# Self-attention of a decoder layer: first loads in halves, SyncE in source order, keys and values of cross-attention from step 2 to 58

## The chip, the cores and the metric

The kernel runs on one core of a Trainium2 chip. Its metric is the device time of one execution in microseconds (us). Each core has TensorE (PE, matrix products), VectorE (DVE), ScalarE (ACT), GpSimd (POOL) and SyncE (SP), which here only issues DMA transfers. Each of these runs its instructions in one fixed order. Where an instruction waits, all that is behind it on that engine waits too, and this holds for the DMA issues of SyncE and GpSimd as well.

## The reference, cut to what matters

All is fp32, with 8 batch rows of 256 tokens and 1024 features.

```python
def reference(x, ctx, pos, mask, ...):
    x = layernorm(x + self_attention(x))            # 32 heads of 32, 8 key/value heads, rope, causal
    x = layernorm(x + cross_attention(x, ctx, pos, mask))   # 32 heads of 128, 8 key/value heads, rope by pos
    x = layernorm(x + ffn(x))                       # a router with 256 slots, top 8
    return x

def self_attention(h):
    q, k, v = h @ wq.T, h @ wk.T, h @ wv.T
    q, k = q * cos + rotate_half(q) * sin, k * cos + rotate_half(k) * sin
    att = softmax(q @ k.T / sqrt(32) + causal)      # 4 query heads share a key head
    return (att @ v) @ wo.T

def cross_attention(h, ctx, pos, mask):
    q, k, v = h @ Wq, ctx @ Wk, ctx @ Wv
    q, k = rope(q, table[pos]), rope(k, table[pos])
    att = softmax(where(mask == 0, -1e9, q @ k.T / sqrt(128)))
    return (att @ v) @ Wo
```

## The kernel before

**Stages.** The kernel has three: self-attention with its layer norm, cross-attention with its own, and the feed-forward part. The change touches the first. In it, cross-attention's keys and values, which need only ctx, are also made, so that TensorE has work while softmaxes run.

**Steps.** Self-attention is a loop of 64 steps, s = 8b + c, for batch row b and group c of four query heads. A step issues, in the order of the source: the weighted sum of the group (`weighted`, L332, in odd steps, for the pair of steps s-1 and s together); the scores of the next step (`scores`, L266, with the softmax of L283 on DVE, L288 and L294 on ACT, and the transposes L299 and L303 on DVE); the query projection of step s + 2 (`project` L207 with `rope` L217 to L220); and one part of `others`: for c < 4 the output projection of the row before (`project_out`, L366), else keys and values of the next row (L207 and L236), and for c of 5 and 6 the turning of the finished row for the next stage (L390). For row 0, c < 4 makes the keys and values of row 1. Values go through DRAM to be laid out anew: `values` writes sa_v rows on ACT's queue, `load_values` (L311) reads them back on SyncE.

**Cross-attention's products in the loop.** From step `KV_BEGIN` to `KV_END` (L32), each step has four products out of 224, which are 4 quarters of 512 tokens by 4 pairs of key/value heads by 14. A pair's product is made by seven products instead of eight, in the order p1, p2, p6, p5, p3, p7, p4, once for keys (L744, and L738 for the turned form) and once for values. p6 and a later one use sums of weights. Those are made on GpSimd: `sums_of_inputs` loads two halves of weights into "ws" (L428, 2 buffers), `run` combines them (four L416) and stores two sums to DRAM (L439), from where SyncE loads them like any weight (L108). `steps` (L478 and L479) says in which step each of these events stands. An event e loads its own half and combines the half of event e-1. `load_all_positions` (L670 for the gathers of the rope tables, L688 to L696 for the positions, made on DVE) and `xa_context(0)` (L629 to L636: ctx and its sums) stand at step KV_BEGIN - 2. `xa_tables` (L704 to L713) turns the tables.

**Buffers.** Weights for all of this share a ring of 9 buffers of 512 KB, and `self.weights` (L108) issues the load on SyncE where the source takes a buffer. xT, the input of a row, has two buffers of 1 MB, sa_v 2, sa_wo (output weights, `load_out`, L357) 4.

**What sets the order.** A scheduler (Tile) places the instructions of an engine by its own costs, except on the engines that `manual_schedule` names: these keep the order of the source. Before, these are TensorE and GpSimd (L97), so SyncE's loads stand where the scheduler puts them. `load_x` (L161) needs a buffer that row b - 1 has been read from for the last time.

**The prologue.** Before the loop: the first keys' weights and xT of row 0 (L178 to L179), then keys, query, values and scores for the first steps (L492 to L504).

Of the kernel before, what the change touches and what calls it, by code (L numbers as in the profile page):

```python
# [8 lines left out]
F32 = mybir.dt.float32  # L9
# [6 lines left out]
DRAM = bass.MemoryType.DRAM  # L16
PE = mybir.EngineType.PE
POOL = mybir.EngineType.Pool

P = 128  # L20
B, S, E = 8, 256, 1024
NT = B * S // P
KC = E // P
# [5 lines left out]
SA_D, SA_KV = 32, 8  # L29
SA_SCALE = 1.0 / SA_D ** 0.5  # L30
SA_STEPS = B * KC
KV_BEGIN, KV_END = 4, 60  # L32

XA_H, XA_KV, XA_D = 32, 8, 128
XA_SCALE = 1.0 / XA_D ** 0.5
# [35 lines left out]
class Layer:  # L71
# [16 lines left out]
    def run(self):  # L88
        nc = self.nc
        self.ident = self.const.tile([P, P], F32, name="ident")  # L90
        make_identity(nc, self.ident)
        self.neghalf = self.const.tile([P, 1], F32, name="neghalf")
        nc.gpsimd.memset(self.neghalf, -0.5)
        self.cos = self.const.tile([P, TQ], F32, name="cos")
        self.sin = self.const.tile([P, TQ], F32, name="sin")
        self.wsums, self.kT_d, self.v_d, self.tables_d = {}, {}, {}, {}
        with self.tc.manual_schedule(engines={PE, POOL}):  # L97
            self.self_attention()
        with self.tc.manual_schedule(engines={PE}):
            self.cross_attention()  # L100
# [45 lines left out]
    def self_attention(self):  # L146
# [4 lines left out]
        nc, tc, a, uni, small = self.nc, self.tc, self.a, self.uni, self.small  # L151
        main, early, psum = ExitStack(), ExitStack(), ExitStack()
        sp = self.pool("sa", 1, main)
        ep = self.pool("sa_early", 1, early, side="right")
        p_sc = self.pool("sa_sc", 2, psum, space=PSUM)

        xTs = {}

        def load_x(b):
            xTs[b] = ep.tile([P, KC, S], F32, name="xT", bufs=2)  # L160
            nc.sync.dma_start(out=xTs[b], in_=a["xT"][b])  # L161

        def load_residual(b):
            for t in (2 * b, 2 * b + 1):
# [7 lines left out]
        def load_kv(b, name):  # L172

            for i in range(2):
                src = a[name][:, :, i * P : (i + 1) * P] if name == "sa_wk" else a[name][:, 4 * i : 4 * i + 4, :]
                wkvs[b, name, i] = self.weights([P, *src.shape[1:]], src)

        load_kv(0, "sa_wk")  # L178
        load_x(0)  # L179
        nc.scalar.dma_start(out=rot, in_=a["sa_rot"])  # L180
        nc.scalar.dma_start(out=sin, in_=a["sa_sin"])
        nc.scalar.dma_start(out=cos, in_=a["sa_cos"])
# [1 line left out]
        def signed():  # L184

            ones = sp.tile([P, 1], F32, name="sa_ones")
            nc.gpsimd.memset(ones, 1.0)
            ps = self.mm()
            nc.tensor.matmul(ps[:, 0:1], lhsT=rot, rhs=ones, start=True, stop=True)
            sign = sp.tile([P, 1], F32, name="sign")  # L190
            nc.vector.tensor_copy(sign, ps[:, 0:1])
            nc.vector.tensor_scalar(sin, sin, sign, None, ALU.mult)
# [31 lines left out]
        def keys(b, i):  # L224
            if i == 0:
                kTs[b] = sp.tile([P, 2, S], F32, name="sa_kT", bufs=2)
                if b:
                    load_kv(b, "sa_wk")
            rope(kTs[b][:, i, :], project(wkvs.pop((b, "sa_wk", i)), xTs[b]))

        def values(b, tt):
            if b and tt == 0:
                load_kv(b, "sa_wv")
            ps = self.mm()
            for k in range(KC):
                nc.tensor.matmul(  # L236
                    ps[:, :256], lhsT=xTs[b][:, k, tt * P : (tt + 1) * P],
                    rhs=wkvs[b, "sa_wv", k // 4][:, k % 4, :],
                    start=(k == 0), stop=(k == KC - 1),
                )  # L240
            rows = sp.tile([P, SA_KV * SA_D], F32, name="sa_vrow", bufs=2)
            nc.scalar.copy(rows, ps[:, :256])
            if tt == 0:
                v_d[b] = self.dram.tile([S, SA_KV * SA_D], F32, name=f"sa_v_{b}")
            nc.scalar.dma_start(out=v_d[b][tt * P : (tt + 1) * P, :], in_=rows)
# [3 lines left out]
        def load_query(s):  # L249
            wqs[s] = self.weights([P, KC, P], a["sa_wq"][s % KC])  # L250

        def query(s):
            ps = project(wqs.pop(s), xTs[s // KC])
            qTs[s] = sp.tile([P, S], F32, name="sa_qT", bufs=2)
            rope(qTs[s], ps)
# [49 lines left out]
        def load_values(b, half):  # L305


            v = vs[b, half] = sp.tile([P, BLOCKS, 4 * SA_D], F32, name="sa_v", bufs=2)
            rows = v_d[b].rearrange("(c i) d -> i c d", i=32)[:, :, half * P : (half + 1) * P]
            for i in range(4):  # L310
                nc.sync.dma_start(out=v[32 * i : 32 * i + 32], in_=rows)  # L311
# [87 lines left out]
        def others(s):  # L399


            b, c = divmod(s, KC)
            parts = []
            if b and c < 4:
                parts.append(lambda: project_out(b - 1, c))
            elif c < 4 or 1 < b + 1 < B:
                parts.append([
                    lambda: keys(b + 1, 0), lambda: keys(b + 1, 1),
                    lambda: values(b + 1, 0), lambda: values(b + 1, 1),
                ][c % 4])  # L410
            if b and c in (5, 6):
                parts.append(lambda: turn(b - 1, c - 5))
            return parts
# [61 lines left out]


        n = XA_KV * 2
        steps = [1 + e * 7 // 8 for e in range(n)]  # L478
        steps += [15 + e * (KV_END - 17) // (len(sums) - n) for e in range(len(sums) - n + 1)]  # L479
        made = []  # L480

        def sum_event():
# [6 lines left out]
        self.hp, self.raws = ep, 3  # L489
        products = [part for q in range(NQ) for m in range(XA_KV // 2) for part in self.xa_keys_values(q, m)]  # L490

        signed()  # L492
        keys(0, 0)
        load_query(0)
        load_kv(0, "sa_wv")
        keys(0, 1)
        load_query(1)
        load_x(1)
        load_query(2)
        query(0)  # L500
        values(0, 0)
        query(1)
        scores(0)
        values(0, 1)  # L504
        last = SA_STEPS
        for s in range(last):
            b, c = divmod(s, KC)
            if c == 4:
                load_residual(b)
            if s == KV_BEGIN - 2:  # L510
                self.load_all_positions()
                self.xa_context(0)
            events = [sum_event] * steps.count(s)
            n = NQ * XA_KV // 2 * 14 // (KV_END - KV_BEGIN)
            mine = []
            if KV_BEGIN <= s < KV_END:
                mine, products = products[:n], products[n:]
            elif s == last - 2:
                mine, self.queries = self.queries[:4], self.queries[4:]
            elif s == last - 1:  # L520
                mine = self.queries + more[:3]
                more = more[3:]
            quarter, first = divmod((s - KV_BEGIN) * n, XA_KV // 2 * 14)
            first = first == 0 and KV_BEGIN <= s < KV_END

            def one():
                if mine:
                    mine.pop(0)()

            def event():  # L530
                if events:
                    events.pop()()

            if s == last - 1:

                for _ in range(5):
                    one()
            if s % 2:
                weighted(s, False)
            elif not first and s < last - 2:  # L540
                one()
            if s % 2 == 0 and s + 1 < last:
                scores(s + 1)
            if s + 2 < last:
                query(s + 2)
            while norms:
                norms.pop(0)()
            for part in others(s):
                part()
            event()  # L550
            one()
            if s % 2:
                weighted(s, True)
                one()
                if s + 1 < last:
                    scores(s + 1)
            if c < 2:
                load_values(b, c)
            elif c == 6:
                load_out(b, 0)  # L560
            if b and c == 1:
                load_out(b - 1, 1)
            if b and c == 0 and b + 1 < B:
                load_x(b + 1)
            if s + 3 < last:
                load_query(s + 3)
            while mine:
                one()
            while events:
                event()  # L570
            if first:
                self.xa_tables(quarter)
            left = len(products)
            if KV_BEGIN <= s < KV_END and left and left % (XA_KV // 2 * 14) == 0:
                self.xa_context(NQ - left // (XA_KV // 2 * 14))
            if s == last - 3:
                early.close()
                self.xa_early()
                more = self.xa_query(1)
            if s == last - 1:  # L580
                psum.close()
                self.xa_psum()
# [1009 lines left out]
```

## Time and profile before

| | |
|---|---|
| median of three runs | 3483.88 us (3478.9 to 3484.5) |
| profiled execution, its own time | 3477.49 us |
| its span in the profile | 3475.7 us |
| mean granted TensorE clock | 0.986 |
| TensorE busy | 3373.5 us, 97% |
| DVE, ACT, POOL busy | 2114.2, 1202.3, 1047.0 us |
| bytes over the span | 626.36 MB, mean 180 GB/s |

The profiled execution is one execution, and its time stands 6.4 us below the median. The span is what the trace covers of it. Busy times are sums over instructions, and those of one engine don't overlap. In the views that follow, a timeline row is start, duration, engine, line, operation and, in brackets, the idle time just before with what ended it. A wait row is the waiting engine and line, what it waited for, and total, times and longest in us. PEclk is the clock granted to TensorE, in tenths of full speed in the page and as a fraction of 1 in the table by windows.

The stage of self-attention ends near 1215 us of the span. The first product of cross-attention stands at 100.61 us.

### The profile page before, as it was taken

What the parts mean: (1) busy time and instruction counts of PE and PEld (TensorE: products, weight loads), DVE (VectorE), ACT (ScalarE), POOL (GpSimd) and SP (SyncE); (2) the same over time, 40 slices, a digit from 0 to 9 for tenths busy, and PEclk for the clock granted to TensorE, in tenths of its full rate; (3) what the DMA queues carried; (4) which work ended last, traced back from release to release, by engine and by line L of the source; (5) the groups of instructions that cost most, each with busy time, mean ns of one, the idle gap of its engine ahead of it and who ended that gap; (6) DMA issues with size and microseconds to landing.
All of it is one profiled execution on the core that took longest, in us unless ns stands there. A gap on an engine that the chain in (4) does not pass through costs nothing.

```text
span 3475.7 us, 71117 instructions
## 1 busy us (share of the span) xinstructions
PE 3373.5 (97%) x27811; PEld 2447.3 (70%) x27811; DVE 2114.2 (61%) x6003; ACT 1202.3 (35%) x4030; POOL 1047.0 (30%) x1363
## 2 busy tenths in 40 slices
PE   7999999999999899999999999999999999999996
PEld 6777777777777667767767667676667766776763
DVE  4655655565565555665675566666665667566556
ACT  3434433343333333333323333223332333333224
POOL 4344655666665221121131112112111212121112
PEclk9999999999999999999999999999999999999998
DMA  8568777886887464444544344544434544444452
GB/s 297 194 230 265 264 263 258 284 277 231 286 275 237 169 202 146 131 143 128 170 151 140 125 131 138 158 143 149 138 128 133 162 145 146 134 130 132 129 148 97
DMA packets 269550, 626.36 MB, mean 180 GB/s; under 512 B 28960, under 2 KB 99760, under 8 KB 268192
## 3 DMA queue, kind: packets, MB, share of 16 engines
q1 hardware_dynamic: 194672, 441.00, 38.8%
q0 software_dynamic: 50032, 154.66, 13.7%
q10 hardware_dynamic: 24512, 26.15, 2.2%
q8 instruction: 221, 3.62, 0.4%
q14 instruction: 113, 0.93, 0.1%
HBM read 526.93 MB, written 94.77 MB: 179 GB/s over the span
## 4 chain that ended last, share of the span: by engine, by line
PE 86%; DVE 6%; ACT 3%; DMA 3%; POOL 2%; issue 1%; SPq 0%; POOLq 0%; DVEq 0%; ACTq 0%
PE mm L744 26%; PE mm L950 19%; PE mm L207 7%; PE mm L897 7%; PE mm L366 6%; PE sc L846 6%; PE mm L738 5%; PE sc L332 2%; PE mm L1228 2%; PE sc L266 1%; ACT att L288 1%; PE mm L236 1%; DMA w<-xa_wv_sums 1%; ACT att L294 1%; PE mm L1005 1%
## 5 line engine op out<-in xcount | busy, mean ns | idle before, releaser
L744 PE MATMUL mm<-x1T,w 128*128 128x256 f32 x3584 | 851.8, 381 | 6.6 <-ACT xatt L866 2.1
L744 PEld LDWEIGHTS mm<-x1T,w 128*128 128x128 f32 x3584 | 676.4, 190 | 192.3 <-issue 84.1
L950 PE MATMUL mm<-w,xoS 128*128 128x512 f32 x992 | 449.2, 595 | 0.0
L860 ACT ACTIVATE xatt<-xatt,nmax 128x256 f32<-128x256 f32 x512 | 257.2, 503 | 507.8 <-DVE nmax L855 495.7
L663 POOL DMA_DIRECT2D v<-v x256 | 150.9, 596 | 736.0 <-PE mm L897 618.0
L950 PE MATMUL mm<-w,xoT 128*128 128x512 f32 x744 | 338.1, 596 | 5.3 <-ACT xoT L905 4.1
L950 PEld LDWEIGHTS mm<-w,xoS 128*128 128x128 f32 x992 | 184.9, 190 | 193.1 <-issue 170.9
L207 PE MATMUL mm<-xT,w 128*128 128x256 f32 x1280 | 303.1, 393 | 10.1 <-DMA xT<-in_xT 10.1
L750 DVE TENSOR_TENSOR half<-mm,half 128x256 f32<-128x256 f32 x288 | 119.9, 416 | 300.6 <-PE mm L744 268.3
L207 PEld LDWEIGHTS mm<-xT,w 128*128 128x128 f32 x1280 | 245.1, 195 | 60.3 <-issue 25.9
L897 PEld LDWEIGHTS mm<-xat,v 32*128 32x128 f32 x8192 | 244.3, 187 | 53.4 <-issue 29.3
L916 POOL TENSOR_TENSOR xoS<-xoT 128x512 f32<-128x512 f32 x62 | 79.0, 1274 | 671.8 <-ACT xoT L905 671.5
L897 PE MATMUL mm<-xat,v 32*128 32x128 f32 x8192 | 270.2, 278 | 5.4 <-DVE acc L957 4.4
L288 ACT ACTIVATE att<-att,nmax 128x128 f32<-128x128 f32 (+1 forms) x512 | 225.6, 442 | 127.8 <-DVE nmax L283 127.6
L750 DVE TENSOR_TENSOR raw<-mm,half 128x256 f32<-128x256 f32 x384 | 159.3, 415 | 172.3 <-PE mm L744 125.3
L846 PE MATMUL sc<-kT,qT 128*128 128x256 f32 x1024 | 262.7, 380 | 0.0
L866 ACT ACTIVATE xatt<-xatt,rec 128x256 f32<-128x256 f32 x512 | 231.1, 499 | 88.0 <-DVE rec L864 87.6
L905 ACT COPY xoT<-mm 128x128 f32<-128x128 f32 x512 | 97.9, 276 | 470.7 <-PE mm L897 439.7
L416 POOL TENSOR_TENSOR ws<-ws 128x256 f32<-128x256 f32 x320 | 243.4, 761 | 27.4 <-DMA ws<-in_xa_wk 6.8
L950 PEld LDWEIGHTS mm<-w,xoT 128*128 128x128 f32 x744 | 138.7, 190 | 148.1 <-issue 127.3
L738 PE MATMUL mm<-w,ctxT 128*128 128x128 f32 x1792 | 217.5, 279 | 12.2 <-DMA w<-xa_wv_sums 9.5
L738 PEld LDWEIGHTS mm<-w,ctxT 128*128 128x128 f32 x1792 | 210.8, 194 | 26.3 <-issue 15.6
(230 smaller groups left out, 4853.2 us busy)
## 6 DMA issues: line engine op xcount, KB each, us to landing
w<-xa_wq_sums SPq DMA_DIRECT2D x128, 512.0 KB, 3.5
w<-xa_wo_sums SPq DMA_DIRECT2D x124, 512.0 KB, 3.7
w<-in_xa_wo SPq DMA_DIRECT2D x97, 512.0 KB, 4.2
w<-in_sa_wq SPq DMA_DIRECT2D x64, 512.0 KB, 6.6
sa_wo<-in_sa_wo SPq DMA_DIRECT2D x64, 512.0 KB, 6.1
w<-in_xa_wq SPq DMA_DIRECT2D x64, 512.0 KB, 3.5
v<-v POOLq DMA_DIRECT2D x256, 128.0 KB
w<-xa_wk_sums SPq DMA_DIRECT2D x32, 512.0 KB, 8.0
```

Source lines behind the costliest of these rows:

```text
L207: nc.tensor.matmul(ps[:, :S], lhsT=lhs[:, k, :], rhs=xT[:, k, :], start=(k == 0), stop=(k == KC - 1),)
L288: nc.scalar.activation(att[:, jj, lo:hi], att[:, jj, lo:hi], AF.Exp, bias=nmax[:, i : i + 1], scale=-1.0, accum_out=sums[:, i : i + 1],)
L366: nc.tensor.matmul(ps, lhsT=oTs[b * KC + c][:, tt * P : (tt + 1) * P], rhs=wos[b, half][c // 2][:, c % 2, :], start=(c == 0), stop=(c == K ...
L416: nc.gpsimd.tensor_tensor(out, in0, in1, op)
L738: nc.tensor.matmul(ps[:, t * P : (t + 1) * P], lhsT=rhs[:, k, t * P : (t + 1) * P], rhs=w[:, k, :], start=(k == 0), stop=(k == 3),)
L744: nc.tensor.matmul(ps[:, :S], lhsT=w[:, k, :], rhs=rhs[:, k, :], start=(k == 0), stop=(k == 3))
L750: nc.vector.tensor_tensor(out, in0, in1, ALU.add)
L846: nc.tensor.matmul(sc[:, qt, :], lhsT=qT[:, q0 : q0 + P], rhs=kT[:, b * S : (b + 1) * S], start=True, stop=True,)
L860: nc.scalar.activation(att[:, qt, :], att[:, qt, :], AF.Exp, bias=nmax[:, qt : qt + 1], scale=-1.0, accum_out=sums[:, qt : qt + 1],)
L866: nc.scalar.activation(att[:, qt, :], att[:, qt, :], AF.Identity, bias=0.0, scale=rec[:, qt : qt + 1])
L897: nc.tensor.matmul(banks[i][:, :P], lhsT=v[rows, c, :], rhs=at[rows, c, :], start=(c == 0), stop=(c == BLOCKS - 1),)
L950: nc.tensor.matmul(ps, lhsT=oT[lhs][:, u, off + p * P : off + (p + 1) * P], rhs=w[:, u, :], start=(u == 0), stop=(u == 1),)
```

## The change

It has five parts.

1. SyncE is added to the engines that keep the order of the source. Its loads now stand where the source has them.
2. `load_x` is issued as two halves of 512 KB. In the prologue, half of the first keys' tile (256 KB), half of xT, and the other halves of both come first; then the first two query tiles, the values' weights, the second keys' tile, the third query tile and xT of row 1.
3. TensorE's first products are reordered: keys 0, query 0, scores 0, query 1, values 0 and 1, keys 1; before: keys 0 and 1, query 0, values 0, query 1, scores 0, values 1. Values come ahead of keys for the next row in `others`.
4. `KV_BEGIN, KV_END` go from 4, 60 to 2, 58, with the sums of weights a step earlier. Positions and ctx are thus loaded at step 0, and stand ahead of the first sum's loads in GpSimd's order.
5. Within a step, loads move: `load_values(b + 1, 0)` to the end of step c = 7, and `load_out(b - 1, 1)` and `load_x` behind the products and events of their step.

```diff
-KV_BEGIN, KV_END = 4, 60
+KV_BEGIN, KV_END = 2, 58
...
-        with self.tc.manual_schedule(engines={PE, POOL}):
+        with self.tc.manual_schedule(engines={PE, POOL, SP}):
             self.self_attention()
...
             xTs[b] = ep.tile([P, KC, S], F32, name="xT", bufs=2)
-            nc.sync.dma_start(out=xTs[b], in_=a["xT"][b])
+            for k in range(0, KC, 4):
+                nc.sync.dma_start(out=xTs[b][:, k : k + 4, :], in_=a["xT"][b][:, k : k + 4, :])
...
-        load_kv(0, "sa_wk")
-        load_x(0)
+        for i in range(2):
+            wkvs[0, "sa_wk", i] = self.weights([P, KC, P], None)
+        first_k = wkvs[0, "sa_wk", 0]
+        xTs[0] = ep.tile([P, KC, S], F32, name="xT", bufs=2)
+        for k in range(0, KC, 4):
+            nc.sync.dma_start(out=first_k[:, k : k + 4, :], in_=a["sa_wk"][:, k : k + 4, :P])
+            nc.sync.dma_start(out=xTs[0][:, k : k + 4, :], in_=a["xT"][0][:, k : k + 4, :])
...
                 parts.append([
+                    lambda: values(b + 1, 0), lambda: values(b + 1, 1),
                     lambda: keys(b + 1, 0), lambda: keys(b + 1, 1),
-                    lambda: values(b + 1, 0), lambda: values(b + 1, 1),
                 ][c % 4])
...
-        steps = [1 + e * 7 // 8 for e in range(n)]
-        steps += [15 + e * (KV_END - 17) // (len(sums) - n) for e in range(len(sums) - n + 1)]
+        steps = [e * 7 // 8 for e in range(n)]
+        steps += [13 + e * (KV_END - 15) // (len(sums) - n) for e in range(len(sums) - n + 1)]
...
+        load_query(0)
+        load_query(1)
+        load_kv(0, "sa_wv")
+        nc.sync.dma_start(out=wkvs[0, "sa_wk", 1], in_=a["sa_wk"][:, :, P:])
+        load_query(2)
+        load_x(1)
         signed()
         keys(0, 0)
-        load_query(0)
-        load_kv(0, "sa_wv")
+        query(0)
+        scores(0)
+        query(1)
+        values(0, 0)
+        values(0, 1)
+        load_values(0, 0)
         keys(0, 1)
-        load_query(1)
-        load_x(1)
-        load_query(2)
-        query(0)
-        values(0, 0)
-        query(1)
-        scores(0)
-        values(0, 1)
...
-            if c < 2:
-                load_values(b, c)
+            if c == 1:
+                load_values(b, 1)
             elif c == 6:
                 load_out(b, 0)
-            if b and c == 1:
-                load_out(b - 1, 1)
-            if b and c == 0 and b + 1 < B:
-                load_x(b + 1)
...
             while events:
                 event()
+            if c == 7 and b + 1 < B:
+                load_values(b + 1, 0)
+            if b and c == 1:
+                load_out(b - 1, 1)
+            if b and c == 0 and b + 1 < B:
+                load_x(b + 1)
```

More of the change, by code (lines that the diff above doesn't have):

```diff
@@ L18 @@
 POOL = mybir.EngineType.Pool
+SP = mybir.EngineType.SP
 P = 128
```

## The prediction

> **What bounds the kernel now.** I read the busy table first, then the chain by engine, then TensorE's list of waits, SyncE's, and the timelines at the four places that the diff touches.
>
> ```profile
> PE 3373.5 (97%) x27811; PEld 2447.3 (70%) x27811; DVE 2114.2 (61%) x6003; ACT 1202.3 (35%) x4030; POOL 1047.0 (30%) x1363
> ...
> PEclk9999999999999999999999999999999999999998
> ...
> PE 86%; DVE 6%; ACT 3%; DMA 3%; POOL 2%; issue 1%; SPq 0%; POOLq 0%; DVEq 0%; ACTq 0%
> ```
>
> TensorE works 3373.5 of 3475.7 us. The change removes no product, so only 102 us of idle time and the time at a low clock can move. Where the idle time lies, from TensorE's list of waits (us, times, longest):
>
> ```profile
> PE mm L207 <- DMA xT<-in_xT: 10.1, 1, 10.1
> PE mm L738 <- DMA w<-xa_wv_sums: 9.5, 4, 5.8
> ...
> PE sc L332 <- DVE at L303: 5.1, 1, 5.1
> ...
> PE mm L744 <- DMA w<-xa_wk_sums: 3.6, 1, 3.6
> ```
>
> and SyncE's between 100 and 1180 us:
>
> ```profile
> SPq L161 <- PE mm L207: 119.9, 5, 29.3
> ...
> SPq L357 <- PE mm L366: 92.4, 56, 17.8
> ```
>
> The first load costs 10 us. SyncE stands five times, up to 29 us, at the xT load of the next batch row (L161), until TensorE's last query of the row before has read the buffer. What is queued behind it, product weights above all, is late together. One of the five (TensorE, SyncE, then windows whose PEclk is the granted clock):
>
> ```profile
> 258.08 2.02 PE L738 MATMUL mm<-w,ctxT 128*128 128x128 f32 x16 [1.09 <-DMA w<-xa_wv_sums]
> ...
> 262.88 7.25 PE L738 MATMUL mm<-w,ctxT 128*128 128x128 f32 x48 [1.92 <-DMA w<-xa_wv_sums]
> ```
>
> ```profile
> 249.59 0.34 SPq L161 DMA_DIRECT2D xT<-in_xT  x1
> ...
> 251.00 0.88 SPq L108 DMA_DIRECT2D w<-xa_wv_sums  x1
> ```
>
> ```profile
> 250.00:263.00 13.00, 9.99 (x183) 8.77 (x183) 6.47 (x27) 3.11 (x12) 5.62 (x8) 1.00 0.98 355
> 263.00:270.00 7.00, 7.00 (x48) 6.95 (x48) 2.40 (x10) 3.87 (x16) 0.83 (x2) 0.76 0.66 245
> ```
>
> The 1 MB of xT and the late weights share a DMA that is full (0.98 busy, 355 GB/s). Then the clock falls to 0.76.
>
> **The start.** Before, the first matmul of work waits for 1 MB of keys' weights and 1 MB of xT, and the weighted sum of step 1 waits for its softmax:
>
> ```profile
> 13.29 12.65 PE L207 MATMUL mm<-xT,w 128*128 128x256 f32 x48 [10.06 <-DMA xT<-in_xT]
> ...
> 50.46 3.47 PE L332 MATMUL sc<-at,sa_v 32*32 32x128 f32 x96 [5.12 <-DVE at L303]
> ```
>
> After, 0.75 MB (half of one key tile, half of xT) is enough. The DMA moved 59 and 296 GB/s in the first two slices of 3 us, 1.07 MB: first matmul at 6 (5.5 to 7), second halves by 8.3, keys done at 10, query 13.5. Rope (four DVE rows of 0.42 us) puts the first scores at 15.5, not 32.8. They are followed by query(1), two values and keys 1 (4 x 3.46 us), so the second scores come at about 30.5, not 37.3. The next values wait for weights that SyncE now issues in source order, behind the four sa_v loads of row 0 (these wait for both stores of values), pos_i and ctxT. I put their arrival at 41, TensorE idle 6.4 us from 34.6 (from both sides: 0 if sa_v does not hold the queue, 9 if the full DMA shares it out), and a low clock after. Weighted(1) starts at 44 to 46, not 50.46. So about 5 of the 17 us stay, 7 with the cold clock of the 5.12 us wait gone (its 32 projections took 9.41 us; 32 at full clock take 7.17).
>
> Here the Trainium skill, "DMA: Bandwidth & Descriptors", section "Measured (HBM→SBUF, 128 partitions, SWDGE, issued from GpSimd)", speaks against halves: batch DMAs to 1 MiB or more for 75% of peak; "Anatomy of one DMA" gives each about 2.0 us fixed. Four pieces in a row would add some 4 us: first matmul at 10. The trace has 512 KB loads at 383 GB/s between 13 and 26 us, since they overlap; I take nothing for the halves and keep the 4 us for the range.
>
> **The sums on GpSimd.** Cross-attention's products use two sums of weights from their third product (p6) on. GpSimd makes each in two halves through DRAM:
>
> ```profile
> 49.02 1.43 POOL L439 DMA_DIRECT2D xa_wk_sums<-ws  x2 [0.30 <-POOL ws L416]
> 55.14 1.43 POOL L428 DMA_DIRECT2D ws<-in_xa_wv  x2 [4.69 <-issue]
> 56.59 3.14 POOL L416 TENSOR_TENSOR ws<-ws 128x256 f32<-128x256 f32 x4
> ```
>
> A half is load 1.44, combine 3.14, store 1.43 us, and the buffer is free after 4.7 more. The change moves the products two steps earlier, the sums only one. It also puts the position gathers (L670) ahead of the first weights in GpSimd's order: before, those were issued at 1.79, and combined at 11.76. After: positions known on DVE about 38.5 (behind pos_i and the softmax), gathers 4.9, ctxT combines 4.7, first ws issue 2.9, landing 3.5, combine 3.1, store 1.7, then the second half in 4.7 + 1.4 + 3.1 + 1.7, landing and SyncE's load of the sum 5 (the xa_wq_sums row at the end of the stage landed in 4.9) and 4: p6 at about 79. TensorE is there at 70 to 73 (start of step 2 at some 58, one scores, query, third key product, table turns and two products at 1.75): 6 to 9 us of stall. Before, it did p6 at 104; the work in between that after does later (two steps of query, scores, other and weighted) makes 14.9: still 7 ahead.
>
> Of the second pair of heads, the keys' sums follow a v store that waits for the twelfth product: 19.1 us of GpSimd, landing and load against 15.3 us of TensorE's work up to p6: 3.8 stall. The values' sums: 21.4 against 15.3, 6.1 stall, and 1 for the second sum. Clock after these waits about 3. Start together: -7 + 3.8 + 6.1 + 1 + 3 = **+7** (from -8, when GpSimd gets its positions early, to +14). Later pairs have a step more; their stall I set to none.
>
> **The middle.** SyncE in source order meets the xT load at the end of step 8b, when the buffer has long been free. The five groups of stalls go: 258/262 1.09 + 1.92, 415/420 0.16 + 0.40, 565 3.65, 723/732 1.76 + 0.68, 879 5.80: 15.46 us. The clock: windows 263 to 270 at 0.76, 565 to 570 at 0.70, 570 to 580 at 0.81, 879 to 885 at 0.55 lose 1.7 + 1.5 + 1.9 + 2.7, less what is idle in them: 7. The Trainium skill, "TensorE: Matmul & The Clock Gate", "What's actually happening", has the clock halve after one idle window of about 3.4 us and come back after as long a busy one: by that only the waits of 3.65 and 5.80 would cost, some 2 x 1.7, and the middle would gain 19 at once instead of 22.5. The row above has 0.76 after waits of 1.09 and 1.92; I follow the trace.
> Against it: the sa_wo loads (L357, 92 us of SyncE's waits before) are in source order too, ahead of product weights at c = 1; by hand these weights still come with 9 us to spare, in three rows a little less, so +3 to +5 for small new stalls. Values and keys in another order within others(), and half xT loads there, cost nothing: same rows of 3.46 us, both beside TensorE's work. Middle: **-19** (-24 to -10; the end of SyncE's cover would be seen as waits at L744 and L738).
>
> **The end.** With products over at step 58, steps 58 and 59 no longer have 8 products (14 us) between scores and weighted. The end before:
>
> ```profile
> 1166.97 0.40 PE L332 MATMUL sc<-at,sa_v 32*32 32x128 f32 x2 [2.98 <-DVE at L299]
> ...
> 1191.12 3.31 PE L744 MATMUL mm<-x1T,w 128*128 128x256 f32 x8 [1.85 <-DMA x1T<-x1T]
> 1195.31 12.32 PE L744 MATMUL mm<-x1T,w 128*128 128x256 f32 x56 [0.89 <-DMA w<-xa_wq_sums]
> ```
>
> A pair of softmaxes takes some 15 us (the first wait above, and 5.12 at 50.46, are of this kind). The work without products between scores(58) and weighted(59) is query, other, scores: some 9; queries and the four products that step 62 has can't cover it. Before, two such gaps stood at 1167 (4.6 together); I put one more at 3.6. Then sa_wo (4 x 512 KB) stands ahead of the first query sums on SyncE: 2 MB at 370 GB/s is 5.7 us, of which 1.9 hidden: +3.8 (2 to 7). Clock +2. End: **+9** (6 to 13). After it the order is the same on TensorE.
>
> Sum: +7 - 19 + 9 = **-3 us**. The profiled execution (3477.5 us, span 3475.7) is 6.4 below the median; the sum is set against the median: **3481**.
>
> **The rivals.** *Faster, the start's lead kept.* If the positions reach GpSimd by 30 (as pos_u did before, at 31) p6 has no stall and the second pair's sums are early: start -8, sum -18: 3466 (3457 to 3474). For it: pos_i is 8 KB, and DVE is half idle there. Against: SyncE's order puts it behind sa_v.
> *Slower, by GpSimd's sums.* One mechanism: every half sum waits for the store of the one before, so a late first sum carries through all four of the second pair. If the first p6 is not at 79 but at 87 (landings of 6 instead of 4, as 6.2 and 7.3 between stores and loads also stand in the trace), 8 us go in at once and some 8 more at pair two, in part as clock: 3498 (3491 to 3510). It decides from a lateness of about 5 us, since the -3 is then used up.
> *Not what it says:* that SyncE's own order makes no difference because five stalls return at sa_wo instead of xT: middle -4 instead of -19, 3496; I hold it with the slower case.
>
> **How the numbers follow.** About 0.2% (7 us) is what a measurement of this kernel can tell from no change. Forecast 0.44 (3470 to 3493), of which 0.12 faster, 0.25 same, 0.07 slower; faster rival 0.29; slower case 0.27. Faster 0.41, same 0.25, slower 0.34. The range, 3459 to 3503, leaves out 0.08 below and 0.11 above; the forecast's own is 3470 to 3493.
>
> **What would show it.** Right: first L207 at 6; L332 of step 1 at 44 to 46; waits for xa_wk_sums and xa_wv_sums only before 160 us; no SyncE row at the xT load waiting for TensorE; a larger wait at L332 around 1130 to 1170 and for xa_wq_sums at its end. Wrong: sums waits late in the stage (SyncE then holds them), a start without a stall at p6 (GpSimd was not late), or a stage end that is as early as the start's gain (the end costs nothing).

## The result and the profile after

| | before | after |
|---|---|---|
| median | 3481.43 us (8 runs, 3476.85 to 3487.75) | 3494.85 us (8 runs, 3489.9 to 3505.31) |
| ratio to before | 1 | 1.0047 [1.0034, 1.0059], some 16 us slower |
| profiled execution, its span | 3477.49, 3475.7 | 3497.42, 3495.6 |
| mean granted clock | 0.986 | 0.982 |

The change makes the kernel slower by 0.47%. The forecast was 3 us faster. The medians are 13.4 us apart, the ratio makes 16 of it, and the two profiled executions are 19.9 us apart. The working below is made against that pair.

TensorE's list of waits of the kernel after (us in total, times, longest):

```profile
PE mm L756 <- DMA w<-xa_wq_sums: 12.4, 1, 12.4
PE mm L756 <- DMA w<-xa_wk_sums: 10.4, 4, 4.9
PE mm L716 <- DMA w<-in_xa_table,pos_u: 8.1, 8, 2.6
PE mm L244 <- issue: 7.2, 1, 7.2
PE mm L750 <- DMA w<-xa_wv_sums: 6.8, 2, 3.8
...
PE mm L215 <- DMA xT<-in_xT: 1.8, 1, 1.8
```

The 10.1 us at the first xT are down to 1.8, as the change means. In their place stand four waits that before had not, or had small: the query sums at the stage's end (12.4, before 0.9), the turns of the rope tables (8.1, before 0.9 for a gather), the values of step 0 (7.2), and key sums (10.4, before 3.6).

To see in which step time is won or lost, I take the end of the second part of `weighted` in each odd step from TensorE's timeline, and subtract the same end of before. A kernel that is ahead in products is credited 1.76 us for each (a row of four products, 32 matmuls of L756, takes 7.07) and 1.1 for each turn of tables (its row takes 1.12). Negative is ahead of before, in us:

| end of step | after | e5 steps 4-60 | e6 gathers | e10 sums | e8 (e5, end) | e13 all |
|---|---|---|---|---|---|---|
| 7 | -5.2 | -12.9 | -5.2 | -7.0 | -8.5 | -9.1 |
| 9 | +5.7 | -12.9 | +4.4 | -6.6 | -8.5 | -8.8 |
| 15 | +5.2 | -16.7 | +4.1 | -7.1 | -11.1 | -8.8 |
| 17 | +15.8 | -16.7 | +7.2 | -6.6 | -11.1 | -5.9 |
| 57 | +11.1 | -22.1 | -9.1 | -17.1 | -16.3 | -20.6 |
| 63 | +27.6 | -10.3 | +6.2 | -2.1 | -10.2 | -10.3 |
| span | +19.9 | -10.8 | +7.9 | -6.3 | -11.4 | -8.7 |

Each column is one execution. e5, e8 and e12_best have the same source up to step 60, and still e5 and e8 stand 4.4 us apart at step 7 and 5.8 at step 57. So I read no difference between columns below some 6 us; jumps within a column are compared instead.

Three jumps make the kernel after slow: 10.9 us between steps 7 and 9, about 11 at step 17 (of which half comes back at step 19, where before has a wait of its own at its turns), and 16.5 after step 57.

**Steps 0 to 9.** TensorE, then SyncE, then GpSimd, kernel after:

```profile
6.16 9.39 PE L215 MATMUL mm<-xT,w 128*128 128x256 f32 x32 [1.85 <-DMA xT<-in_xT]
17.47 0.94 PE L274 MATMUL sc<-sa_kT,sa_qT 32*128 32x128 f32 x16 [1.91 <-DVE sa_qT L228]
...
44.12 5.74 PE L244 MATMUL mm<-w,xT 128*128 128x256 f32 x16 [7.18 <-issue]
...
80.39 1.97 PE L756 MATMUL mm<-ctxT,w 128*128 128x256 f32 x8 [2.97 <-DMA w<-xa_wk_sums]
...
160.74 3.60 PE L750 MATMUL mm<-w,ctxT 128*128 128x128 f32 x16 [3.78 <-DMA w<-xa_wv_sums]
...
167.39 3.44 PE L750 MATMUL mm<-w,ctxT 128*128 128x128 f32 x16 [3.05 <-DMA w<-xa_wv_sums]
```

```profile
31.12 1.81 SPq L319 DMA_DIRECT2D sa_v<-sa_v  x4
32.98 0.45 SPq L700 DMA_DIRECT2D pos_i<-in_pos  x1
33.48 2.08 SPq L641 DMA_DIRECT2D ctxT<-in_ctxT  x4
35.60 1.89 SPq L109 DMA_DIRECT2D w<-in_sa_wv  x2
```

```profile
42.27 2.13 POOL L682 DMA_INDIRECT w<-in_xa_table,pos_u  x1 [40.43 <-DVE at L311]
...
52.79 2.97 POOL L436 DMA_DIRECT2D ws<-in_xa_wk  x4
61.56 3.13 POOL L424 TENSOR_TENSOR ws<-ws 128x256 f32<-128x256 f32 x4 [5.80 <-DMA ws<-in_xa_wk]
```

Work begins at 6.16 instead of 13.29. GpSimd idles 40 us until positions are there, and combines the first weights at 61.56, before at 11.76. The late sums of the second pair are followed by products at about half speed: 16 matmuls in 3.60 and 3.44 us, in a quiet place 1.95.

**A boundary of quarters.** Kernel after, GpSimd, TensorE, and windows (the number before the last two is the granted clock):

```profile
889.23 2.19 POOL L473 DMA_DIRECT2D xa_wo_sums<-ws  x4
891.72 1.04 POOL L682 DMA_INDIRECT w<-in_xa_table,pos_u  x1 [0.30 <-issue]
```

```profile
884.97 7.07 PE L756 MATMUL mm<-ctxT,w 128*128 128x256 f32 x32
894.62 0.52 PE L716 MATMUL mm<-ident,w 128*128 128x128 f32 x2 [2.58 <-DMA w<-in_xa_table,pos_u]
895.93 0.66 PE L716 MATMUL mm<-ident,w 128*128 128x128 f32 x2 [0.79 <-DMA w<-in_xa_table,pos_u]
```

```profile
895.00:899.00 4.00, 2.07 (x11) 0.90 (x11) 0.87 (x3) 0.80 (x3) 3.67 (x4) 0.50 0.25 79
899.00:912.00 13.00, 13.00 (x143) 10.89 (x143) 2.71 (x7) 1.22 (x3) 9.78 (x13) 0.77 0.80 272
```

The gathers stand in GpSimd's order behind a half sum and its stores. TensorE has done the products at 892 and waits for all four gathers, 4.5 us, then runs at 0.50 and 0.77. Before, the first and the last gather of that quarter, the products and the turns stood like this:

```profile
902.07 1.03 POOL L670 DMA_INDIRECT w<-in_xa_table,pos_u  x1 [0.30 <-issue]
...
905.93 0.95 POOL L670 DMA_INDIRECT w<-in_xa_table,pos_u  x1 [0.30 <-issue]
```

```profile
901.29 7.17 PE L744 MATMUL mm<-ctxT,w 128*128 128x256 f32 x32 [1.20 <-DVE sa_qT L220]
908.30 1.12 PE L704 MATMUL mm<-ident,w 128*128 128x128 f32 x8
```

There too a half sum and its stores come just ahead of the gathers, so it is not their order on GpSimd that differs, but how late GpSimd is against TensorE. The first gather is issued 6.2 us before the products end, in the kernel after 0.3 us before; at the first such boundary (near 344) it is 7.7 and 1.4. Even before, this was close. In the kernel after, each turn that waits starts 1.8 to 2.0 us after the issue of its gather has ended. Before, the last gather's issue ended at 906.88 and its turn started at 908.99, 2.1 us later, so by this estimate some 0.2 us was to spare. At the first boundary it was some 5 (the first gather's issue ended at 353.80, its turn started at 360.49), and at the one near 634 a turn already waited 0.89.

**The end.** SyncE, then TensorE, kernel after:

```profile
1197.26 0.62 SPq L667 DMA_DIRECT2D kT<-kT  x1
1207.47 0.38 SPq L109 DMA_DIRECT2D w<-in_mask  x1
1207.90 2.37 SPq L365 DMA_DIRECT2D sa_wo<-in_sa_wo  x4
1210.31 0.94 SPq L109 DMA_DIRECT2D w<-xa_wq_sums  x2
```

```profile
SPq L109 <- DMA x1T<-w: 9.6, 1, 9.6
```

```profile
1220.08 15.18 PE L756 MATMUL mm<-x1T,w 128*128 128x256 f32 x56 [12.43 <-DMA w<-xa_wq_sums]
```

SyncE stands 9.6 us at the mask's load, until a store of turned rows has landed, then issues 2 MB of sa_wo, and only then the sums that TensorE needs. TensorE goes on 9.8 us after their issue. Before, this was 5.0 us, up to TensorE's row at 1195.31:

```profile
1190.28 0.81 SPq L108 DMA_DIRECT2D w<-xa_wq_sums  x2
```

### The profile page after: what moved, and what is told of

The parts are those of the page before. It is cut to its first block, busy times and chain, and to the rows that moved or that the text cites. A ratio compares the mean times of both kernels' runs of the same rounds, so it can differ in the third digit from the quotient of the medians.

```text
span 3495.6 us, 71087 instructions
## 1 busy us (share of the span) xinstructions
PE 3384.6 (97%) x27811; PEld 2452.5 (70%) x27811; DVE 2109.2 (60%) x6003; ACT 1202.3 (34%) x4030; POOL 1048.8 (30%) x1363
## 4 chain that ended last, share of the span: by engine, by line
PE 65%; DVE 4%; issue 1%; POOL 1%; DMA 1%; ACT 1%; SPq 0%; POOLq 0%; ACTq 0%; DVEq 0%
PE mm L756 22%; PE mm L962 20%; PE mm L909 7%; PE sc L858 6%; PE mm L374 2%; PE mm L1240 2%; PE mm L215 2%; PE mm L750 1%; PE mm L1017 1%; POOL acc L991 1%; PE sc L340 1%; DVE res L991 0%; DVE ln_st L126 0%; PE mm L1257 0%; PE mm L1227 0%
## 5 line engine op out<-in xcount | busy, mean ns | idle before, releaser
L756 PE MATMUL mm<-x1T,w 128*128 128x256 f32 x3584 | 853.7, 382 | 15.3 <-DMA w<-xa_wq_sums 12.4
L756 PEld LDWEIGHTS mm<-x1T,w 128*128 128x128 f32 x3584 | 678.1, 191 | 201.3 <-issue 97.4
L750 PE MATMUL mm<-w,ctxT 128*128 128x128 f32 x1792 | 219.7, 281 | 10.3 <-DMA w<-xa_wv_sums 6.8
```

What stands on the lines that cost most here:

```text
L750: nc.tensor.matmul(ps[:, t * P : (t + 1) * P], lhsT=rhs[:, k, t * P : (t + 1) * P], rhs=w[:, k, :], start=(k == 0), stop=(k == 3),)
L756: nc.tensor.matmul(ps[:, :S], lhsT=w[:, k, :], rhs=rhs[:, k, :], start=(k == 0), stop=(k == 3))
```

## The experiments

Ratios are to before, with their intervals. Theory A: the loss comes from the steps 2 to 58. Theory B: it comes from SyncE's own order.

**e1_sp: before, SyncE in source order, nothing else.**

```diff
-        with self.tc.manual_schedule(engines={PE, POOL}):
+        with self.tc.manual_schedule(engines={PE, POOL, SP}):
             self.self_attention()
```

> The kernel before with one part of the change alone: SyncE keeps the order of the source (loads where the source of before has them). Theory A (the middle was lost at the quarters' boundaries, which the steps 2 to 58 moved; SyncE's order itself is good): the five waits at the xT load go, the middle loses 15 us of idle time and 7 of clock, new stalls of 3 to 5: about 15 us faster than before, 0.9955. Theory B (SyncE's own order holds product weights behind ctxT, sa_wo and xT whatever the steps are): as slow as before or 5 to 10 us slower, 1.000 to 1.003, with waits for xa_wk_sums and xa_wv_sums behind sa_wo or ctxT.

Measured: 1.0099 [1.0082, 1.0116], 3515.19 us. Its waits:

```profile
PE mm L745 <- DMA w<-in_xa_wk: 17.3, 4, 6.4
PE mm L745 <- DMA w<-xa_wk_sums: 13.2, 2, 7.1
PE mm L745 <- DMA w<-xa_wq_sums: 12.0, 1, 12.0
```

Theory A's number for this run is refuted, and B's is too small. With the source of before, the order of the source is much the worse one. The end's wait for the query sums is here too, so it belongs to SyncE's order.

**e3_kv: before, steps 2 to 58 alone.**

```diff
-KV_BEGIN, KV_END = 4, 60
+KV_BEGIN, KV_END = 2, 58
...
-        steps = [1 + e * 7 // 8 for e in range(n)]
-        steps += [15 + e * (KV_END - 17) // (len(sums) - n) for e in range(len(sums) - n + 1)]
+        steps = [e * 7 // 8 for e in range(n)]
+        steps += [13 + e * (KV_END - 15) // (len(sums) - n) for e in range(len(sums) - n + 1)]
```

> The kernel before with steps 2 to 58 and the sums a step earlier, and nothing else. Theory A: the boundaries lose about 8 us each at two of the three quarters, the end loses its filled steps (about 5), and the start loses to late sums about 10: 15 to 25 us slower, 1.005 to 1.007, with waits at the table turns for the gathers near steps 16 and 44. Theory B: only the start and the end lose, 8 to 12 us, no waits at the table turns beyond the 0.9 us of before.

Measured: 1.0062 [1.0047, 1.0076], 3498.99 us. Its first two waits:

```profile
PE mm L704 <- DMA w<-in_xa_table,pos_u: 10.7, 6, 5.2
PE mm L738 <- DMA w<-xa_wv_sums: 9.1, 3, 6.1
```

As theory A had it. The waits at the turns come with the steps, without any change to SyncE.

**e4_nosp: the kernel after, SyncE placed by the scheduler.**

```diff
-        with self.tc.manual_schedule(engines={PE, POOL, SP}):
+        with self.tc.manual_schedule(engines={PE, POOL}):
             self.self_attention()
```

> The changed kernel with SyncE's loads placed by the scheduler again (all other parts kept). Theory A: the waits at the table turns (8.1 us) stay, the xT waits come back (15 us), the end's 12.4 us wait for the query sums shrinks to about 1: within 5 us of the changed kernel. Theory B: 15 us faster than the changed kernel, near the time of before.

Measured: 1.0075 [1.0062, 1.0089], 3504.53 us, some 10 us above the kernel after, where theory A had at most 5. Theory B is refuted: in the changed source SyncE's own order doesn't lose time. The turns wait 12.4 us here, and the query sums 2.2.

**e5_kvback: the kernel after, steps 4 to 60** (the diff of e3_kv the other way round).

> The changed kernel with steps 4 to 60 and the sums where before had them (all other parts kept). Theory A: start 7 us ahead of before and kept, no waits at the table turns, no xT waits; the end still waits for the query sums behind sa_wo (up to 12): 10 to 20 us faster than the changed kernel, 0 to 10 us faster than before, 0.997 to 1.000. Theory B: the middle stays as slow as in the changed kernel, 5 to 10 us above before, 1.002 to 1.003.

Measured: 0.9976 [0.9967, 0.9985], 3470.15 us: faster than before, and some 24 us faster than the kernel after. Two of its waits:

```profile
PE mm L756 <- DMA w<-xa_wq_sums: 12.9, 1, 12.9
...
PE mm L716 <- DMA w<-in_xa_table,pos_u: 1.0, 1, 1.0
```

Against before it came as theory A had it (0 to 10 us faster), against the kernel after by more than its 10 to 20 us. It settles which part costs. The rest of the change is worth 8 us, and the steps 2 to 58 cost 24 within it. In the table, the start's lead of 12.9 is kept, and the jumps at steps 9 and 17 are gone. That of the end is not.

**e6_gather: the kernel after, gathers of quarters 1 to 3 one step earlier.**

```diff
             left = len(products)
+            if KV_BEGIN <= s < KV_END and left > n and left % (XA_KV // 2 * 14) == n:
+                self.load_positions(NQ - left // (XA_KV // 2 * 14))
...
-        self.load_positions(q)
+        if q == 0:
+            self.load_positions(q)
```

> The changed kernel with the gathers of the rope tables of quarters 1 to 3 one step earlier in GpSimd's order. If the quarters' boundaries lose time because GpSimd reaches the gathers late (they stand behind a half sum, and TensorE's turns wait 3.6 us near 344 and 4.5 us near 894, with the clock at half after both), the 8.1 us of waits go, and 5 to 8 us of low clock with them: 10 to 16 us faster than the changed kernel. Rival: the gathers are held by the ring of weights, not by GpSimd; then they take a buffer earlier, a weight comes later, and the time stays within 4 us.

Measured: 1.0014 [1.0004, 1.0024], 3485.42 us, 9 to 12 below the kernel after. The turns near 344, with what stands before them:

```profile
335.11 7.07 PE L759 MATMUL mm<-ctxT,w 128*128 128x256 f32 x32
342.02 1.12 PE L719 MATMUL mm<-ident,w 128*128 128x128 f32 x8
```

No wait is left at any of the turns. From step 15 to 57 the kernel wins 13.2 us on before instead of losing 5.9. By the times, the gain is 9 to 12 of these 19 us. That GpSimd came late to the gathers was the cause of these waits, not the ring of weights.

**e7_sums: the kernel after, the sums of step 0 ahead of the gathers.**

```diff
+            events = [sum_event] * steps.count(s)
             if s == KV_BEGIN - 2:
+                while events:
+                    events.pop()()
                 self.load_all_positions()
                 self.xa_context(0)
-            events = [sum_event] * steps.count(s)
```

> The changed kernel with the first half sum on GpSimd ahead of the gathers and of ctx's sums, as before had it. If the start is lost to GpSimd's chain of half sums, one half (about 9 us) leaves the chain: the waits of 2.97 and 1.31 at the first p6 go, those of the second pair (1.23, 3.78, 3.05) shrink, and the lead of some 5 us at the end of step 7 is kept through step 9: 8 to 11 us faster than the changed kernel. Rival: the positions, which come at 42 us behind sa_v on SyncE, set it alone; then the chain starts as late as before and under 3 us are won.

Measured: 1.0030 [1.0018, 1.0043], 3489.59 us. That is some 5 us below the kernel after, but the two intervals overlap, so the times alone do not show a gain. The two waits at the first p6 are gone, as expected. Those of the second pair stayed (3.56 and 2.41 for the values' sums), and the jump at step 9 with them: the first half sum was not the bottleneck of the second pair.

**e10_sums2: as e7_sums, and the first sixteen sums one more step earlier.**

```diff
-        steps = [e * 7 // 8 for e in range(n)]
+        steps = [max(0, e * 7 // 8 - 1) for e in range(n)]
```

> The changed kernel with the first sixteen half sums one more step earlier, so that sums and products have both moved two steps, and those of step 0 ahead of the gathers. If the start's loss is the sums' lag of two steps where before it was three, the second pair's waits (3.78 and 3.05 for the values' sums, 1.23 for the keys') go with the clock after them, and the loss of about 11 us between the end of step 7 and that of step 9 falls under 3: 10 to 14 us faster than the changed kernel. Rival: GpSimd is busy all the time there, so that an earlier place changes little: under 4 us.

Measured: 0.9989 [0.9981, 0.9996], 3474.25 us, about 20 below the kernel after, 14 below e7_sums. Its first three waits:

```profile
PE mm L758 <- DMA w<-xa_wq_sums: 11.3, 1, 11.3
PE mm L244 <- issue: 6.9, 1, 6.9
PE mm L758 <- DMA w<-xa_wk_sums: 5.0, 1, 5.0
```

No wait for the values' sums is in the list, and the jump of 10.9 us at step 9 is now 0.4. The lag between a sum and its product was the cause: it had been three steps and is two in the change. The jump at step 17 went too, though the gathers kept their step: with the sums earlier, GpSimd issues the first of them at 319.8 instead of 341.4, in time for the turns. The waits at the last boundary stayed (4.4 us). So this run and e6_gather win back in part the same loss, and their gains can't be added.

**e11_ctx: the kernel after, positions and ctx behind step 0's values.**

```diff
-            if s == KV_BEGIN - 2:
-                self.load_all_positions()
-                self.xa_context(0)
...
             for part in others(s):
                 part()
+            if s == KV_BEGIN - 2:
+                self.load_all_positions()
+                self.xa_context(0)
```

> The changed kernel with the positions' and ctx's loads behind step 0's values, so that the two loads of the second row's values' weights stand ahead of the 2 MB of ctx on SyncE. If ctx is what makes the wait of 7.2 us at the values of step 0, it falls under 2 us and the low clock after it goes; but the gathers and the sums come no earlier, so that the first p6 waits longer: 0 to 6 us faster than the changed kernel by the time, and about 9 us ahead of it at the end of step 1. Rival: the wait is for the sa_v loads' stores, at the head; then it stays at 7.

Measured: 1.0055 [1.0040, 1.0070], 3496.21 us: as the kernel after. SyncE and TensorE:

```profile
30.50 1.81 SPq L319 DMA_DIRECT2D sa_v<-sa_v  x4
32.36 0.93 SPq L109 DMA_DIRECT2D w<-in_sa_wv  x2
33.33 0.43 SPq L700 DMA_DIRECT2D pos_i<-in_pos  x1
33.80 3.47 SPq L641 DMA_DIRECT2D ctxT<-in_ctxT  x4
```

```profile
37.94 3.69 PE L244 MATMUL mm<-w,xT 128*128 128x256 f32 x16 [1.63 <-DMA w<-in_sa_wv]
47.74 5.13 PE L215 MATMUL mm<-xT,w 128*128 128x256 f32 x16 [4.69 <-DMA w<-in_sa_wq]
```

The wait of 7.2 us was ctx's 2 MB ahead of the values' weights: it falls to 1.63 with sa_v still ahead of them. But the next query's weights now come behind ctx and wait 4.69. The 2 MB are only moved, and so is the wait; the lead at step 1 was 7.0 us, not 9, and the 2 us that it has on the kernel after are within what two executions differ by.

**e8_end: e5_kvback, mask and the last sa_wo loads behind the first query sums.** `load_mask(0)` leaves `xa_early`.

```diff
-            elif c == 6:
+            elif c == 6 and b + 1 < B:
                 load_out(b, 0)
...
             while events:
                 event()
+            if s == last - 2:
+                load_out(b, 0)
+                self.load_mask(0)
```

> The run with steps 4 to 60 (e5_kvback), and at the end of the stage the mask and the last sa_wo loads behind the first query products' weights. If the 12.9 us wait for the query sums comes from SyncE's order alone (mask waiting for the store of the turned rows, then 2 MB of sa_wo ahead), it falls to under 2 us and 10 to 14 us are won: 0.993 to 0.995 of before. Rival: the DMA is full there and the bytes are the limit; then the wait stays above 6 us, and at most 6 are won.

Measured: 0.9956 [0.9940, 0.9972], 3466.07 us. TensorE at the end:

```profile
1170.86 4.72 PE L758 MATMUL mm<-x1T,w 128*128 128x256 f32 x16
1179.73 8.83 PE L758 MATMUL mm<-x1T,w 128*128 128x256 f32 x32 [4.14 <-DVE raw L764]
1192.02 5.42 PE L758 MATMUL mm<-x1T,w 128*128 128x256 f32 x24 [3.46 <-DVE bias L696]
```

The wait of 12.9 is gone, and 7.6 us of others took its place: DVE, behind the last softmax, and the bias that is made from the mask. After step 57 it loses 6.1 us, e5_kvback 11.8. The intervals of the two runs overlap, so a gain over e5_kvback is not shown by the times; the trace has 5.7 us of the expected 10 to 14. SyncE stands as long as ever, now at a load of kT:

```profile
SPq L669 <- DMA x1T<-w: 9.4, 1, 9.4
```

What went is the 2 MB between that stand and the sums. So the rival (the bytes are the limit) has its number, at most 6 us, but not its wait.

**e12_best: as e8_end, with the mask ahead of the sa_wo loads** (the two added calls in the other order).

> Steps 4 to 60 with the rest of the change, and at the end of the stage the mask behind the first query sums but ahead of the last sa_wo loads. In e8_end the bias, made from the mask, held TensorE 3.5 us; with the mask 2 MB earlier this goes: 2 to 4 us faster than e8_end, about 0.9945 of before, and the fastest of all. Rival: the wait that ended on DVE there (4.1 us, softmax of the last step) takes it up: as e8_end, within 2 us.

Measured: 0.9962 [0.9948, 0.9976], 3467.68 us: as e8_end. The bias's wait went, and waits for weights of 2.8 and 4.0 us came. The rival holds, if with another wait than it named.

**e9_three: the kernel after with the edits of e6_gather, e7_sums and e8_end.**

> The changed kernel (steps 2 to 58) with all three: gathers a step earlier, first half sum ahead of the gathers, mask and sa_wo behind the query weights at the end. If these three name what the steps 2 to 58 cost, it is 25 to 35 us faster than the changed kernel, below before (0.995 to 0.998). If something else in the shift costs, it stays above 3480.

Measured: 0.9983 [0.9975, 0.9991], 3474.03 us, 21 below the kernel after, where 25 to 35 were expected. It still jumps by 10.5 us between steps 7 and 9, which e7_sums doesn't mend and e10_sums2 does.

**e13_all: the kernel after with the edits of e6_gather, e10_sums2, e11_ctx and e12_best.**

> The changed kernel, steps 2 to 58, with all that the runs point to: sums two steps earlier, ctx behind step 0's values, gathers a step earlier, mask and sa_wo behind the query sums. If these four are the whole price of the steps 2 to 58, it reaches e12_best within 5 us (0.994 to 0.996 of before). If it stays 8 us or more above e12_best, part of the price is in the steps themselves: the softmaxes at the end with no products to cover them, and products that come before their sums can be made.

Measured: 0.9959 [0.9945, 0.9972], 3465.76 us. It reaches e8_end and e12_best; the three can't be told apart, and each beats both kernels. So, within the some 6 us that these times leave open, what the steps 2 to 58 cost is in the places of the sums, the gathers and the loads around them, not in the products' steps as such. No run shows a gain from the shift itself; steps 4 to 60 with the edits of e6_gather and e10_sums2 were not run.

## Why the prediction was wrong, point by point

**The start, +7: right, in part by errors that offset each other.** Measured +5.2 at the end of step 15. First matmul 6.16 (forecast 6), first scores 17.5 (15.5; the first 32 projections took 9.39 instead of 7), the wait at the values 7.2 (6.4), weighted(1) at 49.8 (44 to 46; the values before it took 5.74 instead of 3.46), first p6 at 80.4 (79) with 4.3 us of waits (6 to 9), lead after step 7 5.2 (7), second pair 10.9 (13.9 with its clock). The forecast's own sum at the first p6 doesn't close: 104 less 79 less 14.9 is a lead of 10, not 7. One cause was named wrong: I put the values' wait to sa_v and ctx together, and e11_ctx shows it to be ctx.

**The middle, -19: wrong by 25 us, and this step failed.** From step 15 to 57 it measured +5.9. What the forecast took away did go: the xT load no longer waits for TensorE, and of the 15.5 us that TensorE waited for product weights and sums in before, between the ends of steps 13 and 57, one wait of 4.9 is left. The term that failed is "+3 to +5 for small new stalls", with "later pairs have a step more; their stall I set to none". I asked of each product when its sum comes, but not what else moves with KV_BEGIN: the boundaries of the quarters went from steps 18, 32 and 46 to 16, 30 and 44, and the gathers there were put at nothing. At two of the three GpSimd reaches them some 6 us later against TensorE's products than before, where the last one had, by my estimate, only some 0.2 us to spare. The waits at the turns were 8.1 us, and TensorE ran at 0.50 to 0.77 after them; taking them away (e6_gather) turned +5.9 into -13.2 in the profiled pair, that is 19 of the 25. Another 4.9 is the wait for key sums at 616 behind four sa_wo loads, which I did name and priced too low.

The shift is not the whole of the error. With the steps of before (e5_kvback) the middle won 5.4 us, or 9.2 counted from step 13, ahead of the first of the five stalls; in e13_all it won 11.8, and in e9_three, the most, 16.1. TensorE waits some 22 us in e5_kvback between the ends of steps 13 and 57, 25 in before: its waits for weights and sums fell from 15.5 to 3.3, but waits for DVE and 4.5 us with no cause in the trace ("issue") stand in their place. So the forecast's 19 us were not reached in any run. Why these other waits came is open.

**The end, +9: right in sign, mis-sized.** Measured +16.5. The term "+3.8 for sa_wo ahead of the sums" became a wait of 12.4, before 0.9. The 2 MB was there, but I missed SyncE's 9.6 us at the mask's load just ahead of it. The rest, 5.0 from step 57 to 61, was near the 3.6 of the forecast and its clock, but by luck: the waits of the weighted sums for DVE, which I said would grow, were 3.8 us (before 4.6), and it was those of the scores that grew, from 1.4 to 3.8.

**After the stage, 0:** in this pair of executions 7.7 us come back later (27.6 to 19.9). In e5, e6, e8 and e13 the same stretch stays within 2 us, in e10 it gives back 4, so I can't put it to the change; its cause is open.

**The rivals.** The slower case gave 3498 by GpSimd's late sums, and GpSimd's lateness is indeed what costs: 10.9 us at the second pair's sums (in the forecast already), and the gathers. But its trigger, the first p6 at 87 instead of 79, did not come: it was 80.4. So its number is near by luck. The faster rival named the positions' arrival; e7_sums and e10_sums2 show that the lag of the second pair decides, whatever the first p6 does. The third, five stalls coming back at sa_wo, gave 3496, the nearest of all. SyncE does stand longer there: from 250 to 1140 us it waits 142.7 us for TensorE at sa_wo loads, before 60.7. But behind them TensorE waits only the 4.9 us at 616, so this too is not the path of the loss.

On the clock, the trace again stands against the rule of the Trainium skill that I weighed ("TensorE: Matmul & The Clock Gate", "What's actually happening", about 3.4 us of idle time): no wait at 894 is longer than 2.58, and the windows after it have 0.50 and 0.77. Here four waits, 4.5 us in all with 0.5 to 0.7 us of work between them, were enough. The halves cost nothing that shows: the first matmul of work is at 6.16, not at the 10 that the forecast kept for a fixed time of each transfer. (Its 383 GB/s between 13 and 26 us were not those of 512 KB loads alone: by the order of issue the 1 MB of xT of row 1 was among them.)

**What stays open.** e1_sp loses 34 us by SyncE's order in the source of before, and the kernel after without SyncE's order is some 10 us slower than with it. Which moved load of part 5, or whether the halves and the new order of the first products, makes the difference was not tried by itself. Why GpSimd falls some 6 us behind TensorE at the boundaries is shown only so far that earlier sums (e10_sums2) bring it back at the first of them.

## What to carry to other kernels

When a group of work is shifted by some steps in a loop whose steps differ, list everything that is placed relative to it (gathers, sums, table turns, the loads at its boundaries) and read the slack of each in the trace, from the landing of a transfer and not from the end of its issue. No list of waits shows it. Here the gathers of two boundaries had some 5 and 0.2 us to spare, and GpSimd fell some 6 us further behind. A lag between producer and consumer in steps is a buffer of time: shorten it only by as much as the producer's chain leaves. And a wait that goes by reordering one queue is won only if what stands ahead of the needed transfer afterwards is not waiting for something slower.

## What the runs showed of the hardware that was not expected

A store of 512 KB on ACT's queue (turned rows, issued at 1194.76) held SyncE's mask load until 1207.47, over 12 us, with about 2.8 MB of SyncE's loads issued beside it. In before the mask's load left 4.2 us after the same store's issue (1178.66 to 1182.81), with as much beside it. With the mask moved, the same store held a load of kT instead, for 9.4 us (e8_end) and 7.7 (e12_best). What made the difference is open.

TensorE stopped for 1.80 us in the middle of a score row near 680 us in the kernel after, and 0.97 near 318, with no wait in the trace ("issue"), both with several MB of SyncE's loads issued in the 13 us before; before has no such row at the scores. The cause was not tried.
